# Layer 1 of a two-layer mixture-of-experts network: twelve strips routed alone instead of eight, and two beside tiles instead of six

## The chip, the cores and the metric

The kernel runs on one core of one Trainium2 chip. The metric is the time of one execution on the device, in microseconds (us); for the kernel before it is the median of ten runs. The core has five engines with instruction queues of their own: TensorE (PE), VectorE (DVE), ScalarE (ACT), GpSimd (POOL) and SyncE (SP, which here issues most transfers). Each queue is worked through in order.

## What is computed

The input is x, 2 x 256 x 56 x 56 in float32: 6272 tokens of 256 channels. There are two layers. Each has a mixing step and then a mixture of eight experts with two experts per token. In layer 0 the mixing step is attention over a 7 x 7 window. In layer 1, which the change touches, it is this, cut to what matters:

```
out1 = relu(batch_norm(conv3x3(ln_c(x), ternary(w1))))
out2 = batch_norm(conv3x3(out1, ternary(w2)))
x = x + relu(out1 + out2)

t = to_tokens(x)
xf = ln_t(t)
logits = xf @ gate_w + gate_b
top2_vals, top2_idx = top_k(softmax(logits), 2)
out = 0
for e in range(8):
    h = gelu(xf @ W1[e] + b1[e])
    out = out + weight_of(e) * (h @ W2[e] + b2[e])
x = from_tokens(t + out)
```

W1[e] is 256 x 512 and W2[e] is 512 x 256. The second batch norm needs the statistics of the whole convolution, so nothing of the routing below can begin before the convolution has ended.

## The kernel before

**Strips and tiles.** The tokens are cut into 14 strips of 448 (eight image rows each, and in a strip 4 blocks of 112 tokens). In the mixture each strip is first routed: the two best experts of each token are found, and the token's normalised row is written, once for each of the two, into a table `xs` in HBM that is sorted by expert. Then tiles of 256 rows of one expert are read from that table and pass through the expert's two matrices; a tile's results are scattered into a second table `ys` at each token's place. At the end each strip gathers its tokens' two results, adds them up with their weights and writes the output. Layer 1 has 64 tiles: 41 full ones and 23 of 128 rows.

**What one strip's routing does.** `residual` (L2110 to L2150) fetches the strip's saved tokens from HBM (`back`, L2115, on SP), forms the batch norm and the sum with the first output on DVE (L2121), the relu on ACT into `nr` (L2125), eight transposes on PE (L2142) and the add of `back` on DVE (L2150). `norm` takes the token statistics on DVE (`token_stats`, L713 to L726), a square root on ACT (L722), scales into the strip's row buffer `u` on ACT (L736), transposes it on PE (L783), copies it on ACT (L788) and forms the logits on PE (L799) and DVE (L808). `settle` then works on a batch of one strip (0 to 3) or two (4 and 5, 6 and 7, and so on): the two best experts by DVE (L826 to L853), the place of each token among its expert's on PE (`rk`, L860 to L863), and the row's position `pos` on DVE (L872 to L877). Last come eight indirect transfers per strip, issued on POOL (L887), that write the rows into `xs`.

**Alone and beside.** `early_strips` routes strips 0 to 7 (`FIRST[1]` is 8) as a pipeline of up to three strips with nothing beside them. `late_strips` routes strips 8 to 13 in small steps that `beside1` calls between the matmuls of the tiles, four calls per tile. A strip that is routed beside tiles is `paced`: it stops at more places, and its transposes use two half-size PSUM tiles. A buffer `u` is held until its rows have been sent; layer 1 has five (`U_BUFS`). `back` has two buffers, and a strip beside tiles fetches the next strip's `back` together with its own.

**Plan, fence and first tiles.** How many of the first 20 tiles each expert gets is known once strips 0 to 7 are counted, because only as many tiles are taken as those strips fill for certain (`EARLY`). `tiles(0)` computes this plan on DVE (L941 to L1016). `fence` issues a small transfer on POOL that reads `xs` (`some`, L2161); it waits until all rows of the early strips have landed. `experts1` then fetches the weights of three tiles (L1096, on SP, 1154 KB each; four buffers), SP waits for the fence, and the rows of four tiles are fetched (L1085). In `experts_in_order` a tile j is worked on like this: `turn` transposes its rows on PE (L1106) and copies them on ACT (L1110), `first` makes the first product on PE (L1138) and the gelu on ACT (L1145), `second` the second product on PE (L1157) and the bias add on DVE into one of five `y` buffers (L1167), and POOL scatters `y` into `ys` (L1169, two transfers for a full tile). Tile 20 and those after it use plans that need all strips (`last_plans`).

**Order of the queues.** In this part the order of SP, DVE, PE and ACT is the order in which the program is written out (`manual_schedule`). In the built program POOL's queue holds 64 row writes, the fence, the scatters of five tiles, and then row writes of strips 8 to 13 mixed with scatters.

Of the kernel before, what the change touches and what calls it, by code (L numbers as in the profile page):

```python
# [11 lines left out]
F32 = mybir.dt.float32  # L12
# [10 lines left out]
B, C, H, W = 2, 256, 56, 56  # L23
# [19 lines left out]
TT = NQ  # L43
# [11 lines left out]
R_ID, R_EX = C, C + 1  # L55
FAR = 1 << 20
NEVER = -3e38
U_BUFS = (4, 5)

T_BASE, T_FULL = 0, E  # L60
T_UPTO = T_FULL + 2 * NREG
# [3 lines left out]
COMPS = 4  # L65
DEN = HEADS * NT // TT
FIRST = (10, 8)

EARLY = tuple(max(0, (TOP * NT * n - E * (G - 1)) // G) for n in FIRST)
X_FIRST = 3  # L70
# [562 lines left out]
def metaformer(ctx: ExitStack, tc: tile.TileContext, a: dict, out: bass.AP, flag):  # L633
# [112 lines left out]
    def routing(layer, wp, tp, ps):  # L746
# [18 lines left out]
        def norm(i, src, late=False):  # L765


            eng = nc.vector if late else small_eng
            paced = layer == 1 and i >= FIRST[1]
            rstd, nmr = yield from token_stats(tp, src, eps5, layer == 1 or late, paced)  # L770
            row = rows[i] = tp.tile([TT, NTT, RW], F32, tag="u", name="u", bufs=U_BUFS[layer])
            u = row[:, :, :C]
            eng.memset(row[:, :, R_EX + 1 :], 0.0)
            eng.tensor_copy(row[:, :, R_ID], ids[:, i * NTT : (i + 1) * NTT])
            if paced:
                yield
            scaled(u, src, rstd, nmr)
            yield
            ut = tp.tile([P, KC, NT], F32, tag="ut", name="ut", bufs=1)
            for k in range(KC):  # L780
                pu = ps.tile([P, 512], F32, tag="aux", name="pu")
                for t in range(NTT):
                    nc.tensor.transpose(  # L783
                        pu[:, t * TT : (t + 1) * TT],
                        u[:, t, k * P : (k + 1) * P],
                        ident[:TT, :TT],
                    )
                nc.scalar.copy(ut[:, k, :], pu[:, :NT])  # L788
            if layer == 0:
                eng.tensor_tensor(src, src, u, ALU.add)  # L790
                nc.sync.dma_start(x_mid[i], src)
                yield
            elif paced:
                yield
            lg = lgs[:, i * NTT : (i + 1) * NTT, :]
            pl = ps.tile([TT, NTT, E], F32, tag="pl" if layer and ps.wide else "aux", name="pl")
            for t in range(NTT):
                for k in range(KC):
                    nc.tensor.matmul(  # L799
                        pl[:, t, :],  # L800
                        ut[:, k, t * TT : (t + 1) * TT],
                        gate[:, k, :],
                        start=k == 0,
                        stop=k == KC - 1,
                    )
            if layer == 1:
                yield
                nc.vector.tensor_tensor(lg, pl, bcast(gate_b, 1, [TT, NTT, E]), ALU.add)  # L808
            else:
                nc.vector.tensor_copy(lg, pl)  # L810
            yield
# [436 lines left out]
    def finish(steps):  # L1248

        while True:  # L1250
            try:
                next(steps)
            except StopIteration as end:
                return end.value
# [494 lines left out]
    with mid:  # L1749
# [336 lines left out]
        with ExitStack() as both:  # L2086
# [14 lines left out]
                True,  # L2101
            )

            backs = {}

            def residual(i):

                b, s = STRIPS[i]
                r = X[b, s]
                paced = i >= FIRST[1]  # L2110
                nr = tp.tile([P, KC, NT], F32, tag="nr", name="nr", bufs=1)
                for at in (i, i + 1)[: 1 + paced]:
                    if at not in backs and at < len(STRIPS):
                        backs[at] = tp.tile([TT, NTT, C], F32, tag="back", name="back")
                        nc.sync.dma_start(backs[at], x_mid[at])  # L2115
                back = backs[i]
                for at in range(1 + paced):
                    for o in range(KC):
                        ro = r[:, o, :].rearrange("p (h w) -> p h w", w=W)
                        if not at:  # L2120
                            nc.vector.scalar_tensor_tensor(  # L2121
                                ro, ro, scale2[:, o : o + 1], inner(b, s)[:, :, o], ALU.mult, ALU.add
                            )
                        if at or not paced:
                            nc.scalar.activation(  # L2125
                                nr[:, o].rearrange("p (t h w) -> p t h w", h=SR, w=TW),
                                blocks(ro),
                                AF.Relu,
                                bias=shift2[:, o : o + 1],
                            )  # L2130
                    if paced:
                        yield
                wide = 2 if paced else NTT
                halves = []
                for t in range(NTT):
                    if not t % wide:
                        pt = ps.tile(
                            [TT, wide, C], F32, tag="aux" if paced else "pt", name="pt"
                        )
                        halves.append((slice(t, t + wide), pt))  # L2140
                    for k in range(KC):
                        nc.tensor.transpose(  # L2142
                            pt[:, t % wide, k * P : (k + 1) * P],
                            nr[:, k, t * TT : (t + 1) * TT],
                            ident,
                        )
                yield
                xt = XT[b, s][:TT]
                for at, pt in halves:
                    nc.vector.tensor_tensor(xt[:, at], pt, back[:, at], ALU.add)  # L2150
# [12 lines left out]

            def early_strips():

                n = FIRST[1]
                jobs = {}
                ready = iter(())
                for i in range(n + 2):
                    young, old = i - 1, i - 2  # L2170
                    if young in jobs:
                        next(jobs[young])
                    finish(ready)
                    if young == 0:
                        next(jobs[young])
                    if i < n:
                        jobs[i] = strip(i)
                        next(jobs[i])
                    if young > 0 and young in jobs:
                        next(jobs[young])  # L2180
                    steps = iter(())
                    if old in jobs:
                        finish(jobs.pop(old))
                        for q in BATCHES:
                            if q[-1] == old:
                                steps = settle(q)
                    for _ in range(3):
                        next(steps, None)
                    if old == 0:
                        finish(steps)  # L2190
                    if young in jobs:
                        next(jobs[young])
                    ready = steps
                finish(ready)
                plan, n_early = tiles(0)
                plans1.append(plan)
                fence()
                return n_early

            def late_strips():  # L2200

                jobs = {i: strip(i) for i in range(FIRST[1], len(STRIPS))}
                jobs[FIRST[1] - 1] = iter(())
                settling, sending = iter(()), iter(())
                for i in range(FIRST[1], len(STRIPS) + 2):
                    here, young = (jobs.get(q, iter(())) for q in (i, i - 1))
                    steps = (
                        (here, young, settling),
                        (here, settling),
                        (here, here),  # L2210
                        (young, settling),
                        (settling, settling),
                        (here, here, young, young),
                    )
                    for at in range(6):
                        for it in steps[at]:
                            next(it, None)
                        next(sending, None)
                        yield
                    for q in BATCHES:  # L2220
                        if q[-1] == i - 2 and q[0] >= FIRST[1]:
                            sending = chain(sending, settling)
                        if q[-1] == i - 1 and q[0] >= FIRST[1]:
                            settling = settle(q, True)
                planned = last_plans()
                sending = chain(sending, settling)
# [35 lines left out]
            route = late_strips()  # L2262
            with tc.manual_schedule(engines=ENGINES):
                n_early = early_strips()
                next(experts1)
                nc.sync.value_load(fences[0])

                route_ps.close()
# [145 lines left out]
```

## Time and profile before

| | us |
|---|---|
| median of 10 runs | 1759.92 |
| lowest and highest of them | 1751.06, 1765.33 |
| the profiled execution | 1760.62 |
| its span in the profile | 1758.7 |
| PE busy in the span | 1489.5 (85%) |
| DVE, ACT, POOL busy | 976.0, 709.7, 653.6 |
| last matrix operation of the second convolution starts | 1143.28 |
| first row write of layer 1 | 1173.30 |
| last row write of strips 0 to 7 | 1259.61 |
| first tile's transposes start | 1267.99 |

All times on an axis are from the start of the span. A row of the timeline gives the start, the duration, the engine, the line (L), what is written and what is read, and how often; in brackets stands how long the engine had been idle before and what ended that idle time. A group of equal instructions that follow each other is one row. Matmuls are pipelined, so the advance from one row's start to the next says more about PE than the durations, which overlap. "issue" means a time in which the engine waited for nothing that the profile shows. A row of stretches gives the busy time of each engine in each, with the number of instructions, then PE's granted clock as a share of full speed, the busy share of the DMA engines and what they moved in GB/s.

### The profile page before, as it was taken

How to read it: one execution, taken by the hardware profiler on the slowest of the kernel's cores; microseconds unless marked ns; L12 is line 12 of the kernel's file. 1: busy time of each engine (PE TensorE's matmuls, PEld its weight loads, DVE VectorE, ACT ScalarE, POOL GpSimd, SP SyncE). 2: the span in 40 equal slices, each digit the busy share in tenths (PEclk: the TensorE clock that was granted, in tenths of full speed). 3: DMA queues.
4: the chain of work that ended last, by engine and by line, in shares of the span. 5: the costliest groups of instructions: out<-in, count | busy, mean ns of one | idle time of the engine just before them, and what ended most of it. 6: DMA issues, size and time to landing. Idle time of an engine off the chain costs nothing. (4 is left out here: it accounts for less than half of the span.)

```text
span 1758.7 us, 25834 instructions
## 1 busy us (share of the span) xinstructions
PE 1489.5 (85%) x8612; PEld 1167.2 (66%) x8612; DVE 976.0 (55%) x2694; ACT 709.7 (40%) x1370; POOL 653.6 (37%) x664
## 2 busy tenths in 40 slices
PE   6999988999878967894899979957199999999953
PEld 3555655555557856783688768846188888898842
DVE  4457756466744436864899888677135421111146
ACT  2545343353433424643445262244066343333312
POOL 2111435253443773443134323426515742222210
PEclk9999998899989989997899989955599999999975
DMA  7122325122267867975753000033566778888868
GB/s 234 45 66 86 115 78 148 44 79 65 61 194 225 290 225 254 328 247 163 196 157 105 1 0 1 1 87 102 194 201 235 259 263 298 276 286 286 284 172 284
DMA packets 91886, 291.77 MB, mean 166 GB/s; under 512 B 20487, under 2 KB 35803, under 8 KB 80416
## 3 DMA queue, kind: packets, MB, share of 16 engines
q1 hardware_dynamic: 66736, 231.79, 42.0%
q0 software_dynamic: 21200, 51.82, 8.3%
q10 hardware_dynamic: 3808, 6.42, 1.1%
q8 instruction: 70, 1.15, 0.3%
q14 instruction: 72, 0.59, 0.1%
HBM read 218.51 MB, written 74.20 MB: 166 GB/s over the span
## 5 line engine op out<-in xcount | busy, mean ns | idle before, releaser
L1138 PE MATMUL ph<-ut,w 128*128 128x256 f32 (+1 forms) x1472 | 313.7, 364 | 6.8 <-DMA w<-in_L_experts 5.9
L1157 PE MATMUL py<-w,h 128*128 128x256 f32 x1288 | 301.3, 382 | 1.3 <-DVE y L1167 1.3
L1138 PEld LDWEIGHTS ph<-ut,w 128*128 128x128 f32 x1472 | 252.8, 196 | 35.7 <-DMA w<-in_L_experts 6.8
L887 POOL DMA_INDIRECT xs<-u,pos x224 | 217.6, 972 | 134.8 <-issue 69.6
L1167 DVE TENSOR_TENSOR y<-py,w 128x512 f32<-128x512 f32 (+1 forms) x120 | 76.8, 640 | 343.2 <-PE py L1157 334.3
L1157 PEld LDWEIGHTS py<-w,h 128*128 128x128 f32 x1288 | 244.4, 192 | 34.4 <-DVE y L1167 1.7
L1169 POOL DMA_INDIRECT ys<-y,dest x136 | 135.3, 995 | 229.8 <-DVE dest L1113 149.1
L1145 ACT ACTIVATE h<-ph,w 128x256 f32<-128x256 f32 (+1 forms) x368 | 161.9, 447 | 106.0 <-PE ph L1138 101.2
L1513 ACT ACTIVATE ex<-sc 112x476 f32<-112x476 f32 (+3 forms) x224 | 116.2, 570 | 192.9 <-PE sc L1503 185.3
L1110 ACT COPY ut<-pt 128x512 f32<-128x512 f32 (+1 forms) x120 | 65.2, 543 | 297.9 <-PE pt L1106 297.8
L1831 PE MATMUL pc<-lo,wq 128*128 128x448 f32 x336 | 131.8, 394 | 8.5 <-DVE lo L1806 8.5
L1523 PE MATMUL av<-ex,vals 112*64 112x238 f32 (+3 forms) x896 | 122.8, 396 | 13.4 <-DVE acc L1533 13.3
L1831 PE MATMUL pc<-hi,wq 128*128 128x448 f32 x336 | 130.9, 392 | 1.2 <-ACT hi L1805 1.2
L1169 POOL DMA_INDIRECT ys<-y,to x81 | 82.0, 1012 | 130.5 <-DVE dest L1113 75.1
L1533 DVE TENSOR_TENSOR acc<-av,acc 128x238 f32<-128x238 f32 (+3 forms) x224 | 88.1, 408 | 73.2 <-PE av L1523 71.2
L1228 DVE SCALAR_TENSOR_TENSOR x<-got,wgt,x 112x256 f32<-112x256 f32 x216 | 102.7, 546 | 32.6 <-DMA got<-ys 32.3
L1974 PE MATMUL pc<-hi,wq 128*128 128x448 f32 (+1 forms) x288 | 103.0, 367 | 17.2 <-ACT hi L1941 9.4
L1106 PE MATMUL pt<-ident,xg 128*128 128x128 f32 x434 | 70.8, 283 | 54.1 <-DMA xg<-xs 43.1
L1106 PEld LDWEIGHTS pt<-ident,xg 128*128 128x128 f32 x434 | 55.8, 147 | 79.5 <-DMA xg<-xs 42.9
L1974 PE MATMUL pc<-lo,wq 128*128 128x448 f32 (+1 forms) x288 | 102.1, 364 | 0.2 <-DVE lo L1942 0.2
L1523 PEld LDWEIGHTS av<-ex,vals 112*64 112x64 f32 x896 | 56.0, 140 | 62.0 <-issue 26.4
L1494 PE MATMUL sc<-q_im,keys 32*112 32x238 f32 (+3 forms) x896 | 91.5, 421 | 6.5 <-ACT ex L1513 6.4
(273 smaller groups left out, 2435.9 us busy)
## 6 DMA issues: line engine op xcount, KB each, us to landing
w<-in_L_experts SPq DMA_DIRECT2D x64, 1154.0 KB
w<-in_L_experts SPq DMA_DIRECT2D x56, 641.0 KB
xg<-xs SPq DMA_DIRECT2D x97, 260.0 KB
got<-ys SPq DMA_DIRECT2D x28, 896.0 KB
acc<-in_fresh SPq DMA_DIRECT2D x14, 896.0 KB
xt<-in_x_tok SPq DMA_DIRECT2D x14, 448.0 KB
xr<-in_x_tok SPq DMA_DIRECT2D x14, 448.0 KB
rec<-shares SPq DMA_DIRECT2D x28, 224.0 KB
```

Of the source, the lines that this page charges most:

```text
L887: w = nc.gpsimd.indirect_dma_start(xs[:, :], bass.IndirectOffsetOnAxis(ap=pos[:, j, t0 + t : t0 + t + 1], axis=0), us[t // NTT][:, t % NTT ...
L1106: nc.tensor.transpose(pt[:, k, i * P : (i + 1) * P], d["xg"][:, i, k * P : (k + 1) * P], ident)
L1138: nc.tensor.matmul(ph[:, :g], w1[:, k, f * P : (f + 1) * P], d["ut"][:, k, :g], start=k == 0, stop=k == KC - 1,)
L1145: nc.scalar.activation(d["h"][:, f, :g], ph[:, :g], AF.Gelu, bias=b1[:, f : f + 1])
L1157: nc.tensor.matmul(py[:, i, :], d["h"][:, f, i * P : (i + 1) * P], w2[:, f, :], start=f == 0, stop=f == NF - 1,)
L1169: o = nc.gpsimd.indirect_dma_start(ys[:, :], bass.IndirectOffsetOnAxis(ap=d["to"][:, i : i + 1], axis=0), y[:, i, :], None, bounds_check=T ...
L1228: nc.vector.scalar_tensor_tensor(xt[:, t, :], y[:, t, j, :], wgt[:, j, n : n + 1], xt[:, t, :], ALU.mult, ALU.add)
L1494: nc.tensor.matmul(sc[h // 2][:, h % 2, :nq], keys[g][p, c, tx * TT : (tx + 1) * TT], q_im[p, c, r0:r1, c0:c1], start=True, stop=False,)
L1513: nc.scalar.activation(e[:, :, :nq], sc[j][:, :, :nq], AF.Exp, scale=HD**-0.5)
L1523: nc.tensor.matmul(av[VW * i : VW * (i + 1), :nq], vals[g % 3][:, tx, 2 * c + j, 2 * i : 2 * i + 2, :].rearrange("p a d -> p (a d)"), ex[j ...
L1831: nc.tensor.matmul(pc[:, :NT], wq[:, k, c, dx * C + o * P : dx * C + (o + 1) * P], part[:, :, k, dx : dx + W], start=m == 0, stop=m == 2 * ...
L1974: nc.tensor.matmul(pc[:, : 2 * ns * W], wq[:, k, c, dx * C + o * P : dx * C + (o + 1) * P], part[:, : 2 * ns, k, dx : dx + W], start=m == ...
```

## The change

Layer 1 routes strips 0 to 11 in `early_strips` and only 12 and 13 in `late_strips`; `paced` follows. The counts that the first plan uses are still those after strip 7, and the first part still has 20 tiles. The plan and the fence are moved into the loop of `early_strips`: they are written out as soon as the rows of strip 7 have been issued, ahead of the residual of strip 10. The first weights are asked for in the iteration of strip 11, behind its `back`. A strip fetches only its own `back`, into a single buffer; layer 1 has six row buffers instead of five. In the built program POOL's queue now holds 64 row writes, the fence, 32 row writes, the scatters of five tiles, and then the 16 row writes of strips 12 and 13 mixed with scatters. The numbers of instructions stay.

```diff
-U_BUFS = (4, 5)
+U_BUFS = (4, 6)
...
 FIRST = (10, 8)
+ALONE = 12
...
-            paced = layer == 1 and i >= FIRST[1]
+            paced = layer == 1 and i >= ALONE
...
-            backs = {}
-
             def residual(i):
...
-                paced = i >= FIRST[1]
+                paced = i >= ALONE
                 nr = tp.tile([P, KC, NT], F32, tag="nr", name="nr", bufs=1)
-                for at in (i, i + 1)[: 1 + paced]:
-                    if at not in backs and at < len(STRIPS):
-                        backs[at] = tp.tile([TT, NTT, C], F32, tag="back", name="back")
-                        nc.sync.dma_start(backs[at], x_mid[at])
-                back = backs[i]
+                back = tp.tile([TT, NTT, C], F32, tag="back", name="back", bufs=1)
+                nc.sync.dma_start(back, x_mid[i])
...
             def early_strips():
 
-                n = FIRST[1]
+                n = ALONE
...
                     finish(ready)
+                    if not plans1 and FIRST[1] - 1 in sent:
+                        plan, n_early = tiles(0)
+                        plans1.append(plan)
+                        fence()
...
                         jobs[i] = strip(i)
                         next(jobs[i])
+                        if i == n - 1:
+
+                            next(experts1)
...
                 finish(ready)
-                plan, n_early = tiles(0)
-                plans1.append(plan)
-                fence()
                 return n_early
 
             def late_strips():
 
-                jobs = {i: strip(i) for i in range(FIRST[1], len(STRIPS))}
-                jobs[FIRST[1] - 1] = iter(())
+                jobs = {i: strip(i) for i in range(ALONE, len(STRIPS))}
                 settling, sending = iter(()), iter(())
-                for i in range(FIRST[1], len(STRIPS) + 2):
+                for i in range(ALONE, len(STRIPS) + 2):
...
-                        if q[-1] == i - 2 and q[0] >= FIRST[1]:
+                        if q[-1] == i - 2 and q[0] >= ALONE:
                             sending = chain(sending, settling)
-                        if q[-1] == i - 1 and q[0] >= FIRST[1]:
+                        if q[-1] == i - 1 and q[0] >= ALONE:
                             settling = settle(q, True)
...
             with tc.manual_schedule(engines=ENGINES):
                 n_early = early_strips()
-                next(experts1)
                 nc.sync.value_load(fences[0])
```

## The prediction

> **What bounds the kernel now.** I read the page first (its second part), then the stretches of 20 us around the second layer's routing, then the chain of waits, then the timelines of POOL, PE and DVE there.
>
> ```profile
> PE   6999988999878967894899979957199999999953
> PEclk9999998899989989997899989955599999999975
> ```
>
> Slices of 44 us. PE has one hole, slice 28 (1231 to 1275 us); then it is full until 1680.
>
> ```profile
> 1220.00:1240.00 20.00, 8.43 (x48) 7.93 (x48) 9.66 (x50) 3.14 (x6) 14.42 (x16) 0.50 0.33 94
> 1240.00:1260.00 20.00, 0.00 (x0) 0.00 (x0) 0.00 (x0) 0.00 (x0) 15.13 (x17) 0.50 0.69 262
> 1300.00:1320.00 20.00, 18.85 (x116) 16.39 (x115) 6.62 (x24) 11.53 (x22) 4.54 (x4) 1.00 0.52 179
> 1440.00:1460.00 20.00, 20.00 (x123) 18.23 (x122) 3.48 (x12) 7.99 (x20) 5.83 (x6) 1.00 0.84 297
> ```
>
> Columns: PE, PEld, DVE, ACT, POOL busy, granted clock, DMA share, GB/s. In the hole only POOL works, on 1.24 us per row write. From 1280 PE is the limit at clock 1.00, with the strips from the ninth on beside tiles until about 1390, and tiles alone after that. While strips are routed alone the clock is 0.50 to 0.68.
>
> ```profile
> 1259.61 2.57 DMA xs<-u,pos
> ...
> 1262.81 1.59 DMA some<-xs
> 1264.49 0.28 SPq L1080
> 1265.33 2.62 DMA xg<-xs
> 1267.99 1.13 PE pt L1106 x4
> ```
>
> The chain through the hole: the 64th row write lands, the fence (`some`) lands, SP fetches a tile's rows, PE starts.
>
> ```profile
> 1173.30 1.17 POOL L887 DMA_INDIRECT xs<-u,pos  x1 [30.14 <-ACT ut L788]
> ...
> 1259.61 0.94 POOL L887 DMA_INDIRECT xs<-u,pos  x1 [0.30 <-issue]
> 1262.81 0.60 POOL L2161 DMA_DIRECT2D some<-xs  x1 [2.26 <-DMA xs<-u,pos]
> 1285.90 1.05 POOL L1169 DMA_INDIRECT ys<-y,dest  x1 [22.49 <-DVE dest L1113]
> ```
>
> POOL has been sending since 1173, and its fence waits for landed rows.
>
> ```profile
> 1154.45 1.23 DVE L2150 TENSOR_TENSOR x<-pt,back 112x1024 f32<-112x1024 f32 x1 [2.62 <-issue]
> ...
> 1216.11 1.21 DVE L2150 TENSOR_TENSOR x<-pt,back 112x1024 f32<-112x1024 f32 x1
> ...
> 1237.64 0.17 DVE L1016 TENSOR_TENSOR taken<-end,nt 128x8 f32<-128x8 f32 x1
> ```
>
> The residual adds of strips 0 and 7, and the plan's end: eight strips alone come at (1216.11 - 1154.45) / 7 = 8.81 us each.
>
> ```profile
> 1267.99 1.11 PE L1106 MATMUL pt<-ident,xg 128*128 128x128 f32 x4 [35.87 <-DMA xg<-xs]
> ...
> 1309.67 0.32 PE L2142 MATMUL pt<-ident,nr 128*112 128x128 f32 x1 [0.74 <-ACT nr L2125]
> ...
> 1397.19 0.60 PE L1106 MATMUL pt<-ident,xg 128*128 128x128 f32 x4
> ...
> 1404.53 0.60 PE L1106 MATMUL pt<-ident,xg 128*128 128x128 f32 x4
> ```
>
> PE idles 35.87 us before the first tile. Later a full tile without a strip beside it takes 7.345 us (1397.19 to 1404.53, the next at 1411.88). A strip beside tiles makes PE wait for ACT as well (0.74).
>
> **The change, part by part.**
>
> *Four strips leave the tile phase.* By the start of each tile's transposes, tile 2 begins at 1275.56 and tile 15 at 1397.19: 13 tiles in 121.63 us. Without strips they would take 13 x 7.345 = 95.49. So six strips cost 26.1 us of PE's path, 4.36 each. Of this PE's own instructions are 0.87 (L2142) + 0.77 (L783) + 1.50 (L799) + 0.22 (half a pair's ranks) = 3.36, by their starts; the rest is waiting for ACT, which reloads its function table (1.28 us, twice around each square root). Four strips less: 4 x 4.36 = 17.4 us. At least 4 x 3.36 = 13.4 (were the waits to stay), at most 18.1 (the intervals that strips 12 and 13 will resemble, those of the first pair with nothing overlapping, sum to 8.0 of the 26.1). I take -17.4.
>
> *The four are routed alone, in the hole.* Before, the last rank matmul of the eighth strip's pair ends at 1232.05, 15.94 us after that strip's add. Four more strips at 8.81 are 35.2. The plan (L943 to L1016, 1233.09 to 1237.81, 4.72 us of DVE) stood behind the last strip; now it stands inside the tenth's iteration, ahead of the eleventh strip's residual on DVE, and holds that chain: 4.7 more. PE is done with routing at 1232.05 + 35.2 + 4.7 = 1272. The first tile's transposes stand behind it on PE, and its rows were there at 1268 before: the start moves by +4.0. Bounds: 0 (the plan hides behind PE's matmuls; the rows' chain then ends last), and +8 (every strip at the slowest spacing shown, 9.58, which is 3.1 more, plus 1).
>
> *POOL.* Its first 64 writes stay; they were the hole's end and go at their own pace. They have company now. In 1188.68 to 1215.99, with DVE busy 23.25 of 28 us, 21 intervals averaged 1.30 us; in 1221.01 to 1259.61, with DVE nearly idle, 1.245. If the last 32 take 1.30, the fence is 1.8 us later: rows at 1270, still under 1272, so 0. The Trainium skill, SBUF - State Buffer, "SBUF: two separate sides", speaks against this overlap: GpSimd and certain Vector instructions exclude one another on a shared pair of ports, and a write sent from POOL then starves. By that rule taken whole, POOL would have only the 4.75 us of those 28 that DVE left free, some five writes of 0.94 us, and the fence would come more than 100 us late, with the sum far above zero; the 22 writes that went there disagree, for this mix of instructions.
>
> *Behind the fence on POOL.* The fence's wait (2.26) now has strip 8's writes behind it, then 32 writes in all, then the first tile's scatter. 1264.5 + 32 x 1.25 = 1304.5 (the positions of strips 10 and 11 are known at 1273, in time for the 17th). Tile 0's `y` is ready near 1289 and waits 15 us. There are five `y` buffers, so PE and DVE feel it only at tile 5, near 1325, by when POOL has done tile 0's pair (2.6 us). Cost 0, with 15 us in hand.
>
> *The single `back` buffer.* Each strip's transfer now starts only after the add before it. Its time: after the add that ends at 1155.68 the DMA row shows 117 GB/s in 1156 to 1160 and 4 or less around, which is one strip's 0.46 MB, so it lands within 4.3 us. The next add starts 7.6 us after the last one's end in the mean, 6.7 at the least (1173.56 to 1180.22). Cost 0, 2.3 us in hand. Beside tiles, strip 13's transfer waits on SP for strip 12's add and holds the next tile's row fetch; the two stand a tile apart in the built order, and rows are fetched four tiles ahead: 0.
>
> *Weights.* Their three first transfers move from 1237 to behind strip 11's `back` (near 1250) and take 12 us (339 GB/s in 1237 to 1249): there by 1263. They now share the DMA engines with the last row writes. Between 0 and +2 for the fence; 0 taken, as 1272 covers it.
>
> *Row buffers.* Six instead of five: strip 10 needs strip 4's, sent by 1230; nothing waits.
>
> *After the tiles* (1682 to the end) everything moves as a block.
>
> Sum: -17.4 + 4.0 = **-13.4 us** on the profiled execution's 1760.62 (span 1758.7 and 1.9 around it): 1747.2. The median of the ten runs is 0.7 lower: **1746.5**. With the bounds, -18.1 to -5.4.
>
> **Rivals.**
>
> *Slower: the single buffer.* If under the row writes a transfer landed 9.4 us after the add or later, each of eleven strips would wait 1.8 or more, 20 us in sum: break-even with the gain is near L = 8.8, and at 10 us it gives 1747 + 26 = 1773. For it: the transfers share the engines with row writes and, once, with weights. Against: 4.3 us at most in the profile. 0.06.
>
> *Slower or no change: POOL's backlog.* If row writes beside tiles took 1.8 us or more, POOL would be free at 1322 or later and tile 5 would wait; at 2.5 us (1344.5), some 22 us are lost: 1769. For it: 32 writes stand ahead of all scatters. Against: 1.24 us each beside tiles in 1369 to 1384. 0.05. The port rule cited above would act by this mechanism too, here and in the hole; what the traces bear of it is in that 0.05.
>
> *No change: transfers pace the tiles instead.* Without strips a tile asks for 1.18 MB of weights and 0.27 of rows in 7.35 us, 197 GB/s, and row writes add 93 (0.116 MB per 1.25 us): 290. If DMA gave less, PE would wait for weights and only the start's shift would be left: 1757 to 1764. Against: 300 GB/s in 1400 to 1420 with PE full. 0.11.
>
> *More gain.* The start stays at 1268: 1742. 0.08.
>
> **How the numbers follow.** The forecast has 0.70 and spans 1741 to 1754. Under 0.3% (5.3 us) this kernel's measurement can't tell a change from none. Faster: 0.70 + 0.08 and a little of the transfer case, 0.79. Same: most of that case and some of the backlog, 0.11. Slower: 0.10. The range, 1738 to 1757, takes in the forecast and the gain's upper case with the runs' spread and leaves about 0.18 out, nearly all above.
>
> **What would show it.** The hole on PE is gone: in 1240 to 1260 PE is busy 14 or more at clock 0.5 to 0.7, and the first L1106 (now one line on) waits under 5 us, not 35.87, and for PE's own routing or the rows within 2 us of each other. It starts at 1272 (1268 to 1276). Tile 15 begins near 1384, 13 before 1397. POOL's 32 writes end near 1304, and no DVE `y` waits for `ys`. Tiles end near 1669 instead of 1682. The adds of strips 1 to 11 do not wait for `back`. Wrong it would be if the adds' spacing rose above 10 us, if tiles showed waits on `w` or `xg`, or if the first tile started after 1281.

## The result and the profile after

The changed kernel takes 1744.64 us in the median of 9 runs (1739.11 to 1754.26), the kernel before 1759.81 (31 runs on the same chip, 1751.06 to 1765.33). The ratio is 0.9925, with a 95% interval of 0.9909 to 0.9941. Run again later beside other kernels it was 1748.02 against 1760.42, ratio 0.9925 (0.9902 to 0.9947). The prediction was 1746.5 in 1738 to 1757, and faster.

The second part of the page after, PE's busy tenths and granted clock in 40 slices, now of 43.6 us:

```profile
PE   5999988999877967894799969958789999999953
...
PEclk9999999899989989987899989965589999999975
```

Slices 26 to 29 (from 0; 1134 to 1308 us) read 5, 8, 7, 8, where they read 5, 7, 1, 9: the hole is gone. The clock stays at 0.5 and 0.6 in the first three, as it was with PE idle.

The windows of 20 us of the changed kernel, with the same columns as before (PE, PEld, DVE, ACT, POOL busy, granted clock, DMA share, GB/s):

```profile
1240.00:1260.00 20.00, 14.25 (x71) 12.49 (x72) 15.34 (x69) 10.56 (x22) 13.64 (x15) 0.50 0.72 249
1260.00:1280.00 20.00, 15.02 (x71) 13.13 (x72) 6.31 (x28) 6.84 (x13) 10.10 (x11) 0.59 0.62 203
1280.00:1300.00 20.00, 19.46 (x104) 16.55 (x103) 9.18 (x32) 13.13 (x25) 15.13 (x17) 1.00 0.79 259
1300.00:1320.00 20.00, 19.83 (x121) 17.70 (x120) 2.77 (x13) 11.48 (x22) 14.01 (x15) 1.00 0.80 275
1320.00:1340.00 20.00, 20.00 (x108) 17.53 (x107) 11.44 (x51) 5.80 (x12) 8.84 (x10) 1.00 0.63 215
```

In 1240 to 1260 PE had nothing to do before; now it is busy 14.25 of 20 us there. The DMA share is 0.72, where it was 0.69, and the rate 249 GB/s, where it was 262. From 1280 PE is the limit again, and PE's work for the two strips left beside tiles is done by 1333.

POOL's timeline after, with the last of the 64 writes, the fence, the first write behind the fence, the last of those 32, and the first scatter:

```profile
1256.96 0.94 POOL L888 DMA_INDIRECT xs<-u,pos  x1 [0.31 <-issue]
1265.28 0.60 POOL L2157 DMA_DIRECT2D some<-xs  x1 [7.38 <-DMA xs<-u,pos]
1267.76 0.98 POOL L888 DMA_INDIRECT xs<-u,pos  x1 [1.89 <-DVE most L827]
...
1306.99 0.94 POOL L888 DMA_INDIRECT xs<-u,pos  x1 [0.30 <-issue]
1308.23 1.01 POOL L1170 DMA_INDIRECT ys<-y,dest  x1 [0.30 <-issue]
```

Counted from the stage's start (set below), the last of the 64 writes is issued at 108.2 us, before at 107.6: they end where they did. The fence behind them now waits 7.38 us for rows to land, where it waited 2.26.

PE's timeline after, at the start of the tiles and at tile 15:

```profile
1268.91 0.30 PE L861 MATMUL rk<-hots,before_w 112*112 112x64 bf16 x1 [3.39 <-DVE hots L849]
...
1269.12 0.79 PE L864 MATMUL rk<-hots,all_w 112*112 112x56 bf16 x7
1270.38 1.12 PE L1107 MATMUL pt<-ident,xg 128*128 128x128 f32 x4 [0.46 <-DMA xg<-xs]
1272.42 1.09 PE L1107 MATMUL pt<-ident,xg 128*128 128x128 f32 x4 [0.92 <-DMA xg<-xs]
...
1382.28 0.60 PE L1107 MATMUL pt<-ident,xg 128*128 128x128 f32 x4
```

The idle time before the first tile is 0.46 us, in place of 35.87: the rows come 0.46 us after PE has done the last ranks. Tile 15 starts at 1382.28, before at 1397.19.

Both profiled executions vary ahead of the stage: the routing of strips starts (the first residual transpose of strip 0) at 1152.05 before and 1148.76 after, where the instructions up to strip 1's residual fetch are the same. So I count from that transpose and call it the stage's start; the numbers below are us from it.

| kernel, profiled execution | fence waited | tile 0 starts | tile 0 to tile 15 | tile 15 starts |
|---|---|---|---|---|
| before (8 strips alone) | 2.26 | 115.9 | 129.2 | 245.1 |
| changed (12) | 7.38 | 121.6 | 111.9 | 233.5 |
| changed, run again | 7.45 | 122.1 | 113.2 | 235.3 |
| 10 strips alone | 2.28 | 116.9 | 121.3 | 238.2 |
| 14 strips alone | 3.10 | 137.9 | 104.1 | 242.0 |
| plan apart | 7.51 | 121.9 | 112.7 | 234.6 |
| one weight ahead of the fence | 2.28 | 120.7 | 112.8 | 233.5 |
| plan apart, one weight | 2.27 | 120.3 | 117.9 | 238.2 |
| two `back` buffers | 6.94 | 121.3 | 113.8 | 235.1 |
| plan apart, one weight, two `back` buffers | 2.25 | 120.1 | 111.3 | 231.4 |

From tile 15 to the last product of the tiles it is 287.4 to 288.0 in all of them. Of the 14.4 us between the two spans (1758.7 and 1744.3), 3.3 were won ahead of the stage and 11.6 in it up to tile 15, 0.6 lost from there to the last product, and 0.1 won behind. The stage therefore explains 11.0 us (9.7 in the changed kernel's second profile). The medians differ by 15.2 and 12.4; the runs of one kernel in these sessions spread by 7 to 18 us, and what lies between the stage's gain and those medians was not located.

### The profile page after: what moved, and what is told of

Its sections match the earlier page's. It is cut to its first block, busy times and chain, and to the rows that moved or that the text cites. A ratio compares the mean times of both kernels' runs of the same rounds, so it can differ in the third digit from the quotient of the medians.

```text
span 1744.3 us, 25840 instructions
## 1 busy us (share of the span) xinstructions
PE 1499.5 (86%) x8612; PEld 1177.8 (68%) x8612; DVE 973.9 (56%) x2690; ACT 701.3 (40%) x1362; POOL 655.0 (38%) x664
## 5 line engine op out<-in xcount | busy, mean ns | idle before, releaser
L1805 POOL TENSOR_TENSOR v<-pad 128x928 f32<-128x928 f32 (+1 forms) x28 | 56.7, 2038 | 99.4 <-DVE lo L1807 48.8
```

## The experiments

The experiments ran four at a time, each four on a chip of their own, beside the kernel before. On the chip of the first four the kernel before takes 1861.74 us (19 runs), and their traces hold waits of 10 to 19 us inside the stage, put down to nothing that the profile knows, and no other chip's trace has one; those four are read by ratio, and by intervals that repeat elsewhere. That chip is called the disturbed one, the others the second and the third.

**How many strips alone: ten, and fourteen.** The changed kernel with the constant at 10 or 14. For 10 the three weight fetches go behind the loop, as in the kernel before, where nothing else differs.

```
-ALONE = 12
+ALONE = 10
...
-                        if i == n - 1:
-                            next(experts1)
...
+                next(experts1)
                 return n_early
```

```
-ALONE = 12
+ALONE = 14
```

Ten, on the disturbed chip:

> Ten strips alone, four beside tiles; the plan stays where the changed kernel has it, and the first weights are asked for after the routing. Theory (the hole is a fixed length set by POOL's 64 writes; a strip beside tiles costs PE 4.4 us, a strip in the hole costs nothing until the hole is full): routing ends near 1253, before the rows' chain, and the weights are through before the last row write, so the first tile starts as far behind strip 0's first transposes as in the kernel before (115.9 us, within 1.5) and tiles 0 to 15 take 111.9 + 8.7 = 120.6 us. In sum 8.7 us under the kernel before, 1751. Rival (the gain of the change is in the earlier rows of the late strips, not in PE's time): tiles 0 to 15 keep 112 us and the time is 1746 or less.

Measured: 1851.85 us against 1861.74, ratio 0.9937 (0.9913 to 0.9960), and a stage full of stalls. Fourteen, there:

> All fourteen strips alone. Theory: tiles 0 to 15 lose the last two strips, 111.9 - 8.7 = 103 to 104 us; the routing is past the hole's end, so every further strip moves the first tile by its whole spacing, 2 x 8.8 = 17.6 us: 121.6 + 17.6 = 139 us behind strip 0's first transposes. In sum about 9 us above the changed kernel: 1754. POOL then has 48 row writes behind the fence, until about 1327, ahead of all scatters; tile 5's result is ready near 1340, so nothing waits for that. Rival (the backlog of POOL stalls tiles): tiles 0 to 15 stay at 112 us or more, and the time is over 1760.

Measured: 1854.19 us, ratio 0.9934 (0.9906 to 0.9963). From the fourth on its tiles came every 7.34 to 7.45 us, with 48 row writes ahead of the scatters, so no backlog held them. But its trace, like that of ten, has such waits in the stage. This is ten's chain:

```profile
1222.60 1.97 ACT u L737 x4
1224.57 11.08 another core or an unknown queue
...
1235.67 0.54 ACT ut L789
```

ACT copies a PSUM tile 11 us after everything that the profile knows of it was ready. What that was, was not found. Both were run again on other chips. Ten:

> Ten strips alone, four beside tiles: half of the change. Row chain sets the start: with the routing two strips shorter (2 x 8.7 = 17.4 us less before the tiles than 121.15 for the end of the routing), the first tile can only follow the fence, at 115.5 to 118 after the stage's start. Two strips more between the first sixteen tiles at 4.36 us each: first tile to tile 15 111.9 + 8.7 = 120.6. Tile 15 at 236.5 to 238, 3 to 4 us later than in the changed kernel; ratio to the kernel before near 0.994. If a strip beside tiles costs no more than its TensorE instructions (3.36 us), the stretch is 118.6 instead.

Measured: 1750.78 us against 1759.29 (29 runs), ratio 0.9946 (0.9930 to 0.9962). The first tile of that kernel on PE's timeline:

```profile
1269.08 1.12 PE L1107 MATMUL pt<-ident,xg 128*128 128x128 f32 x4 [12.78 <-DMA xg<-xs]
```

With ten alone PE still waits 12.78 us for rows: the rows set the start, at 116.9, and the two strips more beside tiles make the stretch 121.3. That is 8.1 to 9.4 us over the changed kernel's, 4.0 to 4.7 for a strip, as the prediction had it (4.36). By the times ten is not told apart from the changed kernel (the intervals of the ratios overlap); the difference is read from the traces. Fourteen:

> All fourteen strips alone, none beside tiles. By the prediction's prices (8.81 us for each strip added to the stretch alone, once the cover of the row chain is used up, against what a strip costs between tiles) the start moves by 2 x 8.8 = 17.6 to 139 and the sixteen first tiles shrink from 111.9 to 15 x 7.35 = 110.3 less the gain at the beginning, 104 to 106: tile 15 near 243 to 245, 10 us later than in the changed kernel, time the same as the kernel before within 4 us. If the row writes behind the fence (48 instead of 32, some 60 us of GpSimd) pace the tiles, as the rival of the backlog says, VectorE waits for ys and t0 to t15 stays over 112: time 8 us or more over that.

Measured: 1754.29 us against 1760.42, ratio 0.9978 (0.9961 to 0.9995). The stretch fell by another 9.1 us, and the start rose by 15.8 (7.9 for a strip alone), a little under the price expected. Tile 15 is 6.7 us behind the changed kernel's on the same chip, where 10 were expected, and the time a little better than the 4 us about the kernel before that I had given it. Here the times too tell it from the changed kernel (0.9925, 0.9902 to 0.9947 on the same chip). Its fence waited 3.10 us; its weights were fetched at 115.7, behind the fence. Beyond the point at which routing and rows end together, a strip alone puts 7.9 us on PE's path, and one beside tiles 4.0 to 4.7.

**What holds the start: the plan, or the weights?** The first tile started 5.7 us later than before, where +4.0 was predicted, and the fence waited 5.1 us more. Two suspects stood: the plan in the middle of the strips, and the three weight fetches that had moved among the last row writes. DVE's timeline of the changed kernel, from strip 9's residual add to strip 10's:

```profile
1230.45 1.22 DVE L2146 TENSOR_TENSOR x<-pt,back 112x1024 f32<-112x1024 f32 x1
...
1236.82 0.17 DVE L944 COPY counts<-counts 128x8 f32<-128x8 f32 x1 [2.19 <-PE counts L942]
...
1241.29 0.17 DVE L1017 TENSOR_TENSOR taken<-end,nt 128x8 f32<-128x8 f32 x1
1241.37 1.27 DVE L2117 SCALAR_TENSOR_TENSOR x<-x,scale,pad 128x448 f32<-128x448 f32 x2
...
1245.29 1.23 DVE L2146 TENSOR_TENSOR x<-pt,back 112x1024 f32<-112x1024 f32 x1 [1.83 <-ACT u L737]
```

Two adds are 14.84 us apart, against 8.8 in the mean. DVE waits 2.19 us for the counts, since their matmul stands behind a strip's logits on PE, and then works on the plan for 4.6; strip 10's modulation (L2117) comes after both. To take the wait away, the planning stops once behind the counts' matmul (the first edit), which is issued one iteration earlier than the rest of the plan:

```
+                if part == 0:
+                    yield
...
-                    if not plans1 and FIRST[1] - 1 in sent:
-                        plan, n_early = tiles(0)
-                        plans1.append(plan)
+                    if i == FIRST[1] + 2:
                         fence()
...
+                    if i == FIRST[1] + 1:
+                        first_plan = planning(0)
+                        next(first_plan)
+                    if i == FIRST[1] + 2:
+                        plan, n_early = finish(first_plan)
+                        plans1.append(plan)
```

To take the weights away from the row writes, two of the three fetches go behind the first four row fetches:

```
-        for j in range(AHEAD):
+        before_rows = 1 if layer else AHEAD
+        for j in range(before_rows):
             live[j] = {}
             fetch_weights(j)
         tp, ps = yield
         for j in range(ROWS_AHEAD):
             fetch_rows(j)
+        for j in range(before_rows, AHEAD):
+            fetch_weights(j)
```

Each alone, first on the disturbed chip.

> The changed kernel, with the plan's matrix operation issued right behind the ranks of strips 6 and 7 and the rest of the plan behind the logits of strip 8, where VectorE otherwise waits for TensorE; the fence stays. In the changed kernel the residual adds of strips 9 and 10 lie 14.84 us apart, against 8.35 for those of strips 7 and 8. Theory (the plan holds the routing chain, and the routing's end and the rows' chain both set the start): that spacing falls to about 11, the weights are asked for 4 us earlier and hold the last rows less, and the first tile starts about 4 us earlier, 117.5 us behind strip 0's first transposes: 1740.5. Rival (the rows' chain alone sets the start, at POOL's pace): the spacing falls, the first tile waits longer for its rows, and the start moves by 0.5 us or less: 1744.

> The changed kernel, with only the first tile's weights asked for before the fence and those of tiles 1 and 2 behind the rows of the first four tiles. In the changed kernel the fence waits 7.38 us after the last row write, in the kernel before 2.26. Theory (the weights' 3.5 MB share the DMA engines with the last row writes and delay their landing): the fence's wait falls to 3 to 4.5 us, the rows are there before the routing ends, and the start is set by the routing alone, 0.5 to 1.4 us earlier; tile 1 waits at most 2 us for its weights. Time within 1.5 us of the changed kernel. Rival (the fence waits for something else, such as the 32 writes behind it): its wait stays at 7 us.

Measured: plan apart 1841.58 us, ratio 0.9885 (0.9850 to 0.9921); one weight 1853.5, ratio 0.9954 (0.9928 to 0.9979). The fence of one weight waited 2.54 us, that of plan apart 6.63, so the weights' part showed even there. Stalls moved the starts to 150 and 152, and nothing more is read from them. On the second chip the changed kernel, as a base:

> The changed kernel itself, beside the next three on one chip, as their common base. Its first profile had: add to add of the strips 9 to 10 14.8 us, last of 64 row writes 108.2 us after the stage's start (the first transpose of strip 0), fence issued at 116.5 after a wait of 7.4, first tile's transposes at 121.6, tile 15's at 233.5. Expected again within a microsecond on a chip without stalls, and a ratio to the kernel before of 0.990 to 0.995.

Measured: ratio 0.9925; strips 9 to 10 14.87 us, fence wait 7.45, tile 0 at 122.1, tile 15 at 235.3. It repeats. Plan apart there:

> The plan's counts go through TensorE a strip earlier, and the rest of the plan runs when VectorE has them. All three weight fetches stay ahead of the fence. Theory A (the fence, held by row writes that share the DMA engines with 3.5 MB of weights, sets the start): the hole of 14.8 us between adds 9 and 10 falls to 8.5 to 10, routing ends on TensorE near 116, but the fence still waits 6 to 7.5 us and the first tile starts at 120.5 to 121.6; time as the changed kernel's within 1.5 us. Theory B (the routing alone sets the start): first tile at 116 to 117.5, 4 to 5 us less than the changed kernel.

Measured: 1744.14 us against 1760.42, ratio 0.9911 (0.9890 to 0.9932), not told apart from the changed kernel. The start was 121.9, held by the fence (7.51), as theory A says. But the hole between the adds of strips 9 and 10, which both theories took for gone, was still 14.22 us. PE's and DVE's timelines of that kernel show what came instead:

```profile
1227.63 0.17 PE L942 MATMUL counts<-seen_b,all_w 112*128 112x8 bf16 x1
1230.77 0.98 PE L784 MATMUL pu<-ident,u 112*128 112x112 f32 x4 [2.98 <-DVE place L873]
```

```profile
1241.46 0.17 DVE L1019 TENSOR_TENSOR taken<-end,nt 128x8 f32<-128x8 f32 x1
1241.57 1.23 DVE L2148 TENSOR_TENSOR x<-pt,back 112x1024 f32<-112x1024 f32 x1
```

The counts go through PE at once (1227.63), and PE then stands 2.98 us, released by DVE's reading of the ranks from PSUM (`place<-rk`), a wait the changed kernel does not have there. The plan still runs as one block of DVE, now directly ahead of the add. In the kernel the ranks, the counts and the transposes of `u` share one PSUM tag with two buffers (`aux`). With the ranks in one and the counts in the other, the transposes must wait until DVE has read the ranks, which fits the 2.98 us; it was not tried by itself.

One weight alone, on the third chip:

> One of three layer-1 weight fetches ahead of the fence, nothing else. Theory (the weights on the DMA engines hold back the last row writes): fence wait 2.3 to 2.6 instead of 7.4 us, fence issued at 111 to 112. But the routing ends on TensorE at 121.1 as before, so the first tile starts at 121 to 121.6, no more than 0.6 us earlier, without waiting for its rows. Then the weights and the single residual buffer of strip 12 stand behind each other on SP's queue: first tile to tile 15 117 to 118 as in the run with both edits, so 4 to 6 us slower than the changed kernel. If instead the late weights were free, time as the changed kernel's within 1 us.

Measured: 1750.05 us against 1759.29, ratio 0.9943 (0.9925 to 0.9962). POOL's and PE's timelines:

```profile
1262.57 0.60 POOL L2160 DMA_DIRECT2D some<-xs  x1 [2.28 <-DMA xs<-u,pos]
```

```profile
1271.49 0.79 PE L864 MATMUL rk<-hots,all_w 112*112 112x56 bf16 x7
1272.15 1.09 PE L1107 MATMUL pt<-ident,xg 128*128 128x128 f32 x4
```

The fence's wait is back at 2.28, so the weights were the whole of its 5.1 us: one fetch of 1154 KB did not hold the writes back, three did. It is not the number alone, but what is still in flight at the last writes. SP's timelines of the changed kernel and of ten alone have the same three fetches, asked for at 98.9 and 92.3 us after the stage's start:

```profile
1247.64 2.97 SPq L1097 DMA_DIRECT2D w<-in_L_experts  x3
```

```profile
1244.46 2.67 SPq L1097 DMA_DIRECT2D w<-in_L_experts  x3
```

In the changed kernel the DMA engines are full (share 1.02 to 1.04) in 1254 to 1260 and still at 0.80 in 1260 to 1262, beyond the last write at 1256.96. In ten alone the share falls to 0.41 in 1258 to 1260, ahead of the last write at 1260.20, and the fence waits 2.28.

With one weight ahead of the fence the first tile waits for nothing but PE's ranks, and yet it starts at 120.7, only 0.9 earlier. The second half of the expectation missed: no 4 to 6 us were lost, the stretch was 112.8. The time is not told apart from the changed kernel's.

Both edits together:

> The plan apart as in the run before, and only one layer-1 weight fetch ahead of the fence, the other two behind the first four fetches of rows. Theory A (two chains end nearly together, the rows' and the routing's, and both have to be shortened): fence wait 2.3 to 2.6 us, first tile at 115.5 to 117.5, tile 15 some 4 to 6 us earlier than in the changed kernel, time 4 to 6 us less, less what the late second and third weights cost the first expert change (0 to 3). Theory B (the weights only move their delay behind the rows): the gain is lost again in waits of the first layer products for weights, time within 1.5 us of the changed kernel.

Measured: 1750.32 us, ratio 0.9954 (0.9930 to 0.9977). Start at 120.3 and fence 2.27, as theory A says, but not the 115.5 to 117.5 of it, since the routing is no shorter. And the stretch grew by 4.7, in one tile of 17.31 us instead of 11.49. No gain is left: the interval of the ratio overlaps the changed kernel's on this chip (0.9902 to 0.9947). SP's, DVE's and PE's timelines there:

```profile
1273.78 1.66 SPq L1099 DMA_DIRECT2D w<-in_L_experts  x2
...
1277.34 0.33 SPq L1099 DMA_DIRECT2D w<-in_L_experts  x1
1277.78 0.96 SPq L2117 DMA_DIRECT2D back<-x_mid  x1
```

```profile
1294.02 1.29 DVE L2151 TENSOR_TENSOR x<-pt,back 112x512 f32<-112x512 f32 x2 [16.05 <-DMA back<-x_mid]
...
1307.79 1.29 DVE L2151 TENSOR_TENSOR x<-pt,back 112x512 f32<-112x512 f32 x2 [7.28 <-DMA back<-x_mid]
```

```profile
1298.78 0.60 PE L1109 MATMUL pt<-ident,xg 128*128 128x128 f32 x4
...
1308.54 1.60 PE L784 MATMUL pu<-ident,u 112*128 112x112 f32 x8 [3.74 <-DVE x L2151]
1309.93 4.82 PE L1160 MATMUL py<-w,h 128*128 128x256 f32 x16
...
1316.09 0.63 PE L1109 MATMUL pt<-ident,xg 128*128 128x128 f32 x4
```

The loss is not the weights' lateness but the single `back` buffer, which keeps strip 12's and 13's transfers from being asked for earlier: strip 12's half was issued on SP at 1277.78, within 4 us behind three weight fetches (in the changed kernel behind one), and was there at 1294, and strip 13's, which stands on SP behind a weight fetch that waits for its own buffer, at 1307.8. PE felt the second one. In one weight alone the same order on SP gave strip 13's add a wait of 4.79 us, and that tile took 13.10, 1.6 more. PE's timeline of one weight alone there:

```profile
1302.02 1.20 PE L784 MATMUL pu<-ident,u 112*128 112x112 f32 x8 [1.18 <-DVE x L2149]
1303.05 3.63 PE L1158 MATMUL py<-w,h 128*128 128x256 f32 x16
```

The two timelines tell 5.8 from 1.6. Against the changed kernel's second profile PE reaches these transposes 4.0 us later into the tile with both edits and 1.4 later with one. Behind the longer wait PE's granted clock is 0.72 (1308.5 to 1314.6), and the transposes and the sixteen products lose another 1.8; with one weight it is 1.00 (1303 to 1306.5), and they lose 0.3. Counted from the stage's start strip 12's add came 1.75 us later with both edits, and strip 13's transfer was issued later by as much; why strip 12's half came later was not settled.

**The single `back` buffer.** The kernel before's two buffers and early fetch, put into the changed kernel (and five `u` buffers, to make room), alone and with both edits:

```
-U_BUFS = (4, 6)
+U_BUFS = (4, 5)
...
+            backs = {}
...
-                back = tp.tile([TT, NTT, C], F32, tag="back", name="back", bufs=1)
-                nc.sync.dma_start(back, x_mid[i])
+                for at in (i, i + 1)[: 1 + (i >= ALONE - 1)]:
+                    if at not in backs and at < len(STRIPS):
+                        backs[at] = tp.tile([TT, NTT, C], F32, tag="back", name="back")
+                        nc.sync.dma_start(backs[at], x_mid[at])
+                back = backs[i]
```

> The changed kernel with the kernel before's two buffers for the residual's other half (back) and five instead of six u buffers, so the rival of the single buffer put straight: my theory is that the single buffer costs nothing here (no add waits for it in the changed kernel), so tile 15 at 233.5 to 235.3 and the time within 1 us of the changed kernel. The rival would gain 1 us or more, in the adds of strips 1 to 13. If the sixth u buffer is needed, a wait for it shows in the strips 9 to 11 alone, and the start is later by it.

Measured: 1748.26 us against 1759.29, ratio 0.9940 (0.9922 to 0.9959); tile 15 at 235.1, the adds of strips 7 to 11 within 0.1 us of the changed kernel's. The single buffer costs nothing in the changed kernel, and the sixth `u` buffer gains nothing.

> The plan apart and one weight fetch ahead of the fence, with two back buffers, so that strip 12's half is fetched before the weights. Theory: of the run with both edits the adds of strips 12 and 13 waited 16.1 and 7.3 us for the single buffer, because its transfers stood among the weights that had been moved; with the transfer earlier the stretch from first tile to tile 15 comes back from 117.9 to 112 to 113, the start stays at 120.3, tile 15 at 232.3 to 233.5, time 1 to 2 us less than the changed kernel. If the loss was the weights' own lateness, the first layer products wait for weights and the stretch stays over 116.

Measured: 1744.07 us against 1759.29, ratio 0.9909 (0.9884 to 0.9934). The adds of strips 12 and 13, and the first tile behind the ranks:

```profile
1286.18 1.29 DVE L2156 TENSOR_TENSOR x<-pt,back 112x512 f32<-112x512 f32 x2 [10.79 <-ACT nr L2131]
1298.60 1.29 DVE L2156 TENSOR_TENSOR x<-pt,back 112x512 f32<-112x512 f32 x2 [1.25 <-ACT ut L1113]
```

```profile
1271.90 0.79 PE L864 MATMUL rk<-hots,all_w 112*112 112x56 bf16 x7
1272.56 1.09 PE L1109 MATMUL pt<-ident,xg 128*128 128x128 f32 x4
```

No add waits for `back` any more, and the stretch is back at 111.3. That shows the cause of the 17.31 us tile. Of all the kernels its tile 15 comes first, at 231.4, 2.1 and 3.9 us ahead of the changed kernel's two profiles. By the times it is not told apart from the changed kernel: the ratios' intervals overlap (0.9909 to 0.9941 there).

## Why the prediction was right

The mechanism is the predicted one. Its sum (-13.4) is 2.4 to 3.7 us more than the traces give for the stage at the tiles' end (-11.0 and -9.7 in the two profiles), while the medians came out at -15.2 and -12.4. That the first median lies within 1.9 us of the forecast is therefore partly luck: the stage gained less than was said, and something outside it, not located, made up for that. In the two profiles the start took 1.7 and 2.2 us of the difference, the tile phase 0.1 and 1.4, and the rest lies behind tile 15. By its steps:

- *Four strips leave the tile phase, -17.4.* Measured -17.3 (129.2 to 111.9), -16.0 in the second profile. Half the change (ten alone) gave -7.9, and two strips more (fourteen) -9.1: 4.0 to 4.7 for each, where 4.36 was worked out from tile 2 to tile 15. PE's instructions alone (3.36) would have been too little in each case; the waits went with the strips.
- *Routed alone, +4.0 to the start.* Measured +5.7, and +6.2 in the second profile; it is the term that was mis-sized. By the prediction's own working the ranks should end at 119.95 after the stage's start; they ended at 121.15. Its four strips and plan (35.2 + 4.7 = 39.9) took 41.0, from add to add (64.3 to 105.27): the plan was priced by DVE's work alone, and the wait of 2.19 us for its counts behind a strip's matmuls on PE was left out.
- *Weights, 0 to +2 for the fence, 0 taken.* The fence's wait rose by 5.1, not by 2 at most, and that is shown to be the weights: one fetch instead of three ahead of the fence brings 2.28 back. Asked for earlier (85.3 in the kernel before, 92.3 in ten) they cost nothing: the fence waited 2.26 and 2.28. In fourteen they were asked for only behind the fence (115.7), and it waited 3.10; what the 0.8 there are was not sought. Yet that the end of the routing covers it nearly held: the first tile waited only 0.46 us for its rows (0.97 in the second profile), and started 0.9 earlier where they were on time. Of the 1.7 us by which the start was missed the routing's own end is 1.2, and the rows the rest.
- *POOL's pace in the hole.* The 64th write was issued at 108.2, before at 107.6: +0.6, where up to +1.8 was allowed. DVE was busy 13.88 of the 17 us in 1240 to 1257, and from 1240.65 to 1256.96 the writes follow one another at 1.255 us in thirteen intervals (before, with DVE nearly idle, 1.245). So DVE's work here cost POOL 0.01 us a write. The rule that the prediction takes from the Trainium skill, SBUF — State Buffer, "SBUF: two separate sides", is about Vector instructions in a 2-port mode or with two SBUF inputs only, where the prediction's "taken whole" counts every one of them. No run here tells which of these instructions it would cover.
- *Behind the fence on POOL.* Counted from the stage's start the 32 writes began at 119.0, where 112.5 was said, since the fence was late, and the first scatter stood behind them until 159.5 (1308.23), where 152.5 was said. Tile 0's `y` (written from 1287.56) waited 20 us for it, not 15. It cost nothing, as said: tile 0's pair had gone from POOL by 1310.5, and the sixth tile's `y`, which needs its buffer, was written at 1330.94 and waited only for PE. Four tiles' scatters were through at 1318.3, and PE was full from 1320. There was no backlog with 48 writes in fourteen alone either.
- *The single `back` buffer, 0.* Right: none of the adds waits for it in the changed kernel, and two buffers gain nothing. The rival's mechanism is real all the same. It cost a tile 1.6 and 5.8 us as soon as two weight fetches were moved in front of strip 12's transfer.
- *Transfers pace the tiles.* No: 275 GB/s in 1300 to 1320 with PE at 19.83 of 20, and from tile 9 on 7.34 to 7.35 us for each tile.
- *After the tiles*: 287.4 to 288.0 from tile 15 to the last product, 74.1 and 74.0 behind it; a block, as said.

## What to carry to other kernels

When work moves from beside a full engine into a hole, its price is nothing only until the chains that end the hole meet: here rows and routing met at twelve strips. Ten left 12.78 us of the hole unused, and fourteen paid 7.9 us for a strip that costs 4.0 to 4.7 beside tiles. So work out the end of each chain and put the split where they cross; and price a planning step not by its engine's instructions but by where its first input stands in the other engine's order. A transfer moved to please one waiter stands in front of another on the same queue, and a single buffer that was free of cost shows it first.

## What the runs showed of the hardware

- Row writes of POOL and weight fetches of SP share the DMA engines, and it is the landing that suffers, not the issue: with three fetches of 1154 KB among the last ones, writes went on at 1.25 us, but the fence behind the last one waited 6.94 to 7.51 us for it to land, against 2.25 to 2.28; with one fetch, or with three asked for at 92.3 us after the stage's start instead of 98.9, it waited no longer than before.
- A 448 KB transfer within 4 us behind three such fetches was awaited until 16 us after its issue (1277.78 to 1294.02), where alone it took 4.3 at most (by the kernel before's DMA rate in 1156 to 1160).
- On one of the chips the same kernel takes 1862 us instead of 1760, with single waits of 10 to 19 us that the profile puts down to nothing it knows. All kernels kept their sign by ratio there (0.9885 to 0.9954); fourteen alone came out at 0.9934 there and at 0.9978 elsewhere, with intervals that just meet. The cause is open.
